# Sigmoid attention inside the ternary feed-forward's steps, VectorE's order in them, and the last stage's weights, first norm and routing beside them

## Chip, cores and metric

The kernel runs on one core of one Trainium2 chip. The metric is the device time of the whole kernel in microseconds (us); lower is better. The core has five engines that each work through their own instructions in order: TensorE (PE: matrix products, with weight loads shown apart as PEld), VectorE (DVE), ScalarE (ACT), GpSimd (POOL) and SyncE (SP), whose queue starts most of the DMAs here. An instruction that needs another engine's result waits for it, and so does everything behind it on its own engine.

## What is computed

A net of four layers, each of a cross attention and a feed-forward, all added to one residual `x` of 2048 tokens by 256 features, with `ctx_2048` as the other input of the attentions. The change touches the last three of these eight parts:

```python
def _rmsnorm(x, g):
    return g * (x * jax.lax.rsqrt(jnp.mean(x * x, axis=-1, keepdims=True) + 1e-8))
def _act_quant(x):
    scale = 127.0 / jnp.clip(jnp.max(jnp.abs(x), axis=-1, keepdims=True), 0.0001, None)
    return jnp.clip(jnp.round(x * scale), -128, 127) / scale
def _ternary_quant(w):
    s = jnp.mean(jnp.abs(w))
    return jnp.round(jnp.tanh(w / (s + 1e-8))) * jnp.arctanh(s)
def _linear_bit(x, w, g):
    return jnp.einsum('bsd,od->bso', _act_quant(_rmsnorm(x, g)), _ternary_quant(w))
def _L2_ffn_ref(x, w1, g1, w2, g2, w3, g3):
    h = jax.nn.silu(_linear_bit(x, w1, g1)) * _linear_bit(x, w2, g2)
    return _linear_bit(h, w3, g3)

def _L3_xattn_ref(Q, K, V):          # per batch of 64 tokens
    score = jax.nn.sigmoid(jnp.einsum('bdn,bdm->bnm', Q, K) / sqrt(dk))
    return jnp.einsum('bvn,bnm->bvm', V, score)

def _L3_ffn_ref(...):                # 8 experts of 176, two per token, and a shared one of 352
    scores = jax.nn.softmax(x @ gate_w.T, axis=-1)
    topk_w, topk_i = jax.lax.top_k(scores, 2)
    h = silu(x @ w_gate[e]) * (x @ w_up[e])
    y = sum over e of combine[:, e] * (h @ w_down[e])
    return y + (silu(x @ sw_gate) * (x @ sw_up)) @ sw_down

x = x + _L2_ffn_ref(_layernorm(x), ...)
x = x + _L3_xattn_ref(_layernorm(x), ctx_2048, ctx_2048)
x = x + _L3_ffn_ref(_layernorm(x), ...)
```

## The kernel before

The residual stays on chip as sixteen tiles `xs[i]` of 128 tokens by 256 features, the context as `cs[i]`. Eight stages, named by letters in `STAGES = "ABCDEFGH"`, run one behind the other; each opens its pools of memory on the left or on the right side of SBUF in turn (`side_of`), so that the weights of the next stage are loaded (`weights`, `load_*`) while one stage runs. Stages A to E are not touched. The planner of the language is free to interleave instructions of neighbouring stages where data and buffers allow it.

**Stage F** (`run_F`, L1238) is the ternary feed-forward. Its section has a schedule by hand (`tc.manual_schedule()`): each engine gets the instructions in the order in which they are written. A tile's work is cut into parts, and in step t the loop at L1384 issues each part for tile t minus its lag, so that several tiles are under way at once. In the order of a tile:

- `deviations` (lag -1): mean and variance on VectorE (`b`, `mv`), a small term, and the power -1/2 on GpSimd (`s`).
- `first_sizes` (lag 0): `xk`, the tile less its mean times each of two gains; its largest magnitudes `am`; then `scales` (L1270): a clamp (L1272), a reciprocal (L1274), the factor `sca` for rounding (L1275) and the factor `dqa` for scaling back (L1277).
- `first_rounding` (0) on ScalarE: `xq`, rounded by adding a large number. `first_transposes` (1) on TensorE, `first_copy` (1) on ScalarE: `xT`.
- `hidden_products` (1) on TensorE: `l`, two products of 1024 columns. `gates` (1) on ScalarE: silu, `sl`. `hidden` (2) on VectorE: `h`.
- `squares` (2) on ScalarE: `junk` and the sum `ss`. `gained` (2) on GpSimd: `xr`, `h` times the gain `g3` (L1344). `second_norm` (3): VectorE and a power on GpSimd (`rr`).
- `second_rounding` (3) on VectorE: the largest magnitude `amb` (L1355), `scales` for 128x1, and `hq` (L1358). `second_transposes` (4), `second_copy` (4): `hqT`, `hT`. `output` (4): `op`. `summed` (5) on VectorE: adds into `xs[i]` (L1380).

The banks of PSUM (`xqT`, `l0`, `l1`, `hqT0`, `hqT1`, `op`) are there once each, so a part waits for the readers of its bank of the step before.

**Stage G** (`run_G`, L1397) is the sigmoid attention, tile by tile: norm into `q` on VectorE, transposed context `cT` (copied by VectorE, L1409), scores of two batches of 64 tokens (L1415), sigmoid on ScalarE (L1419), product `gop` (L1425), and the add into `xs[i]` on VectorE (L1428).

**Stage H** (`run_H`, L1451) is the mixture of experts, in four groups of four tiles. `routed` norms and transposes a group, computes the gate products `hgp`, a softmax and the two largest (`softmax_small`, `top2`), and spreads the weights of the experts over `share` in three bf16 pieces; a product with the constant pattern `owner` brings them to the columns (`cb`). The body computes for 14 chunks `pgate` and `pup`, silu, the product `hm`, and collects `hout`. `routed` of the next group is issued whole behind chunk 5. `owner` (a memset and six selections on GpSimd, L1460 to L1464) is built at the head of the stage; H's weights lie on the side that F used.

Of the kernel before, what the change touches and what calls it, by code (L numbers as in the profile page):

```python
# [31 lines left out]
def tile_net(ctx: ExitStack, tc: tile.TileContext, a: dict, out: bass.AP):  # L32
# [31 lines left out]

    beside = []
    pending = []

    def side_of(stage):
        return ("left", "right")[STAGES.index(stage) % 2]


# [1166 lines left out]
    def run_F(w, side):  # L1238
# [3 lines left out]

        if "ternary" in shared:
            with tc.tile_pool(name="Fp0", bufs=1, space=PSUM) as psum:
                for _ in shared.pop("ternary")(side, psum):
                    pass
        at = shared["atanh"]
        t1, t2, t3 = (t.rearrange("p (c n) -> p c n", c=c) for t, c in zip(shared["tern"], (2, 2, 8)))
        with tc.tile_pool(name="Ft", bufs=1, side=side) as tpool, tc.tile_pool(
# [6 lines left out]
            st = [{} for _ in range(NT)]  # L1256

            def deviations(i):

                b6 = pool.tile([P, 6], F32, name="b6")  # L1260
                V.bn_stats(b6, xs[i])
                mv = st[i]["mv"] = pool.tile([P, 2], F32, name="mv")
                V.bn_aggr(mv, b6)
                ve = pool.tile([P, 1], F32, name="ve")
                V.tensor_scalar(ve, mv[:, 1:2], 1e-5, 1e-8, ALU.add, ALU.mult)
                V.tensor_tensor(ve, ve, mv[:, 1:2], ALU.add)
                s = st[i]["s"] = pool.tile([P, 1], F32, name="s")
                G.tensor_tensor(s, ve, mhalf[:, 0:1], ALU.pow)

            def scales(am, s, at_, n, nm):  # L1270

                V.tensor_scalar(am, am, s, 1e-4, ALU.mult, ALU.max)  # L1272
                sc = pool.tile([P, n], F32, name=f"sc{nm}")
                V.reciprocal(sc, am)  # L1274
                V.tensor_scalar(sc, sc, s, 127.0, ALU.mult, ALU.mult)  # L1275
                dq = pool.tile([P, n], F32, name=f"dq{nm}", bufs=4)
                V.tensor_tensor(dq, am, at_, ALU.mult)  # L1277
                return sc, dq

            def first_sizes(i):  # L1280
# [6 lines left out]
                sc, d["dq"] = scales(am, d["s"], at[:, 0:2], 2, "a")  # L1287
                d["xk"], d["sc"] = xk, sc
# [57 lines left out]
            def second_norm(i):  # L1346
                d = st[i]
                V.tensor_scalar(d["ss"], d["ss"], 1.0 / 1024.0, 1e-8, ALU.mult, ALU.add)
                d["rr"] = pool.tile([P, 1], F32, name="rr")
                G.tensor_tensor(d["rr"], d["ss"], mhalf[:, 0:1], ALU.pow)  # L1350

            def second_rounding(i):
                d = st[i]
                am = pool.tile([P, 1], F32, name="amb")
                V.tensor_reduce(am, d["xr"], AX.X, ALU.max, apply_absolute_value=True)  # L1355
                sc, d["dqb"] = scales(am, d["rr"], at[:, 2:3], 1, "b")
# [25 lines left out]

            deviations(0)
            for t in range(NT + 6):  # L1384
                for part, lag in (
                    (summed, 5), (first_transposes, 1), (first_copy, 1), (second_transposes, 4), (second_copy, 4),
                    (hidden, 2), (hidden_products, 1), (gates, 1), (second_norm, 3), (squares, 2), (gained, 2),
                    (first_sizes, 0), (first_rounding, 0), (second_rounding, 3), (output, 4), (deviations, -1),
                ):
                    if 0 <= t - lag < NT:  # L1390
                        part(t - lag)

# [38 lines left out]
    def load_H(wp):  # L1431
# [16 lines left out]
        w["down"] = t  # L1448
        return w

    def run_H(w, side):  # L1451


        with ExitStack() as es:
            cp = es.enter_context(tc.tile_pool(name="Hc", bufs=1, side=side))
            pool = es.enter_context(tc.tile_pool(name="Hw", bufs=2, side=side))
            psum = es.enter_context(tc.tile_pool(name="Hp", bufs=1, space=PSUM))

            owner = cp.tile([96, 1408], BF, name="owner")
            G.memset(owner, 1.0)  # L1460
            for t in range(3):
                rows = owner[32 * t : 32 * t + 32]
                G.affine_select(rows, rows, [[1, 1408]], ALU.is_ge, 0.0, base=0, channel_multiplier=-176)
                G.affine_select(rows, rows, [[-1, 1408]], ALU.is_ge, 0.0, base=175, channel_multiplier=176)  # L1464
            shares = []
            for b in range(2):
                t = cp.tile([96, 512], BF, name=f"share{b}")
                V.memset(t, 0.0)
                shares.append(t)

            def routed(g):

                ids = range(4 * g, 4 * g + 4)
                xnT = norm_T(pool, psum, ids)
                gp = psum.tile([P, 4, 8], F32, tag="tp", name="hgp")
                for j in range(4):
                    for c in range(2):
                        PE.matmul(
                            gp[:, j, :], xnT[:, c, j * P : (j + 1) * P], w["gate"][:, c, :], start=c == 0, stop=c == 1
                        )  # L1480
                sc = softmax_small(pool, gp, 4, 8)
                (s1, s2), _ = top2(pool, sc, 4, 8)
                V.tensor_tensor(s1, s1, s2, ALU.add)
                comb = pool.tile([P, 4, 8], F32, name="comb")
                V.tensor_tensor(comb, sc, s1, ALU.mult)
                tp = psum.tile([P, 4, P], F32, tag="tp", name="combT")
                for j in range(4):
                    PE.transpose(tp[0:8, j, :], comb[:, j, :], ident)
                src = tp[0:8].rearrange("e j t -> e (j t)")
                sh = shares[g % 2]  # L1490
                r = pool.tile([8, 512], F32, name="shr")
# [154 lines left out]
```

## Time and profile before

| | us |
|---|---|
| median of 3 runs | 2878.74 (2876.58 to 2881.87) |
| the profiled execution | 2879.53, its span 2877.8 |
| TensorE, VectorE, ScalarE, GpSimd busy | 2468.2, 1914.5, 1531.7, 1506.4 |
| stages A to E | up to 2346.9 |
| F, from the first tile's statistics | 2346.9 to 2495.3 |
| G | 2495.3 to 2555.2 |
| H | 2555.2 to 2877.8 |

The page gives for each engine its busy time, the span in 40 slices with tenths of busy time, the clock that TensorE was granted, the chain of work that ended last, and groups of instructions by line with the mean duration of one and the idle time before them. The bounds of the stages in the table were read from the chain: the last row of one stage's lines and the first of the next. A stage's limit is read from its own stretch, since a share of the whole span mixes all eight. In the stretches table a row gives start and end, length, and for each engine busy time and number of instructions, then the granted clock and the DMA share. Busy times of one engine can overlap a little where two instructions overlap; start-to-start times add up.

### The profile page before, as it was taken

To read this page: it belongs to the slowest core of one execution; us is meant where nothing else is said; L and a number is where in the kernel's file an instruction comes from. 1 tells how busy PE (TensorE), PEld (TensorE's weight loads), DVE (VectorE), ACT (ScalarE), POOL (GpSimd) and SP (SyncE) were. 2 spreads that over 40 slices of the span, in tenths; PEclk is the share of its full clock that TensorE was granted. 3 is DMA by queue.
4 is the path that set the end of the run, shared out by engine and by line. 5 is a ranking of instruction groups with operands and counts; after the bars stand their busy time and mean duration, and the time that the engine had idled before them with its cause. 6 is when DMAs were issued, how large, how long until landed. Compare 5 with 4: busy or idle time off the path is not lost.

```text
span 2877.8 us, 44432 instructions
## 1 busy us (share of the span) xinstructions
PE 2468.2 (86%) x16072; PEld 1449.1 (50%) x16072; DVE 1914.5 (67%) x3989; ACT 1531.7 (53%) x2145; POOL 1506.4 (52%) x1681
## 2 busy tenths in 40 slices
PE   4989798777778777689999999789888976789999
PEld 2545344344444444346666666556555533445555
DVE  7877554699999999775455455663577669833332
ACT  1657221599999999655555555353345556521110
POOL 4655433588888888665555555311587754400000
PEclk9999899999999999889999999888999988999999
DMA  6553000499999999910000000001443300200000
GB/s 166 128 116 70 23 1 1 106 202 203 202 207 201 204 201 199 186 59 8 15 15 15 8 1 1 30 30 24 103 93 89 92 1 1 76 1 8 8 8 8
DMA packets 610599, 223.70 MB, mean 78 GB/s; under 512 B 547366, under 2 KB 600524, under 8 KB 605772
## 3 DMA queue, kind: packets, MB, share of 16 engines
q1 hardware_dynamic: 607308, 220.07, 35.0%
q8 instruction: 127, 2.08, 0.3%
q10 hardware_dynamic: 3072, 0.79, 0.2%
q14 instruction: 92, 0.75, 0.1%
HBM read 66.91 MB, written 18.87 MB: 30 GB/s over the span
## 4 chain that ended last, share of the span: by engine, by line
PE 50%; DVE 22%; issue 9%; POOL 5%; ACT 2%; DMA 1%; ACTq 0%; DVEq 0%; POOLq 0%; SPq 0%
DVE e L789 11%; PE yp L985 4%; PE ppq L926 3%; PE ppk L926 3%; PE hout L1502 3%; PE vp L914 3%; PE pgate L1523 3%; PE pup L1523 3%; PE sp L944 2%; PE ep L1072 2%; PE op L970 2%; PE hmp L1065 2%; PE sc L759 1%; PE op L495 1%; POOL e L286 1%
## 5 line engine op out<-in xcount | busy, mean ns | idle before, releaser
L813 ACT ACTIVATE ei<-e,nb,sq 128x2048 int16<-128x2048 f32 x256 | 535.4, 2092 | 43.4 <-DVE nb L810 39.7
L823 POOL CAST eb<-ei 128x2048 bf16<-128x2048 int16 x256 | 482.5, 1895 | 116.1 <-ACT ei L813 102.0
L759 PE MATMUL sc<-kT,qz 128*128 128x512 bf16 x1024 | 298.1, 382 | 142.0 <-DVE e L789 139.9
L246 DVE TENSOR_REDUCE negm<-s 128x2 f32<-128x512 f32 (+1 forms) x512 | 300.9, 611 | 130.6 <-PE s L242 127.4
L789 DVE TENSOR_SCALAR_CACHE_REDUCE e<-sc,mx 128x1024 f32<-128x1024 f32 x256 | 326.1, 1274 | 0.8 <-DVE nb L810 0.7
L789 DVE TENSOR_SCALAR_CACHE_REDUCE e<-sc 128x1024 f32<-128x1024 f32 x256 | 312.4, 1220 | 10.5 <-PE sc L759 10.5
L278 ACT ACTIVATE e<-s 128x1024 f32<-128x1024 f32 (+1 forms) x256 | 233.2, 915 | 152.8 <-PE s L274 117.3
L242 PE MATMUL s<-stk,stq 96*128 96x256 bf16 (+1 forms) x1024 | 192.2, 271 | 41.2 <-DMA d3k<-t3k 24.8
L759 PEld LDWEIGHTS <-qz 128*128 128x128 bf16 x1024 | 94.9, 97 | 261.2 <-issue 202.6
L934 POOL TENSOR_TENSOR rwq<-rwq,sin 128x512 f32<-128x512 f32 x64 | 81.1, 1268 | 240.1 <-ACT rwq L931 203.7
L274 PE MATMUL s<-stq,stk 128*128 128x256 bf16 (+1 forms) x1024 | 180.6, 262 | 10.8 <-DMA stq<-nm 5.4
L772 PEld LDWEIGHTS <-vz 128*64 128x64 bf16 x4096 | 123.2, 110 | 114.0 <-issue 113.9
L946 DVE TENSOR_REDUCE mx<-sp 128x4 f32<-128x512 f32 x64 | 44.3, 692 | 192.7 <-PE sp L944 192.7
L772 PE MATMUL av<-eT,vz 128*64 128x128 bf16 x4096 | 164.0, 223 | 7.3 <-DMA eT<-eb 7.2
L87 POOL TENSOR_TENSOR rstd<-ve,mhalf 128x1 f32<-128x1 f32 (+1 forms) x56 | 42.4, 757 | 240.9 <-DVE ve L85 145.9
L931 ACT ACTIVATE rwq<-ppq,dbq 64x512 f32<-64x512 f32 x128 | 87.4, 683 | 148.9 <-DVE rtq L928 148.0
L1533 DVE TENSOR_TENSOR hm<-pup,sl 128x512 f32<-128x512 f32 (+1 forms) x56 | 38.7, 692 | 191.1 <-PE pup L1523 187.4
L242 PEld LDWEIGHTS <-stq 96*128 96x128 bf16 x1024 | 93.6, 101 | 131.9 <-issue 108.6
L296 PE MATMUL o<-e,vmo 128*32 128x256 f32 (+1 forms) x2048 | 151.1, 367 | 7.4 <-POOL e L286 6.0
L1531 ACT ACTIVATE sl<-pgate 128x512 f32<-128x512 f32 (+1 forms) x56 | 33.4, 597 | 219.2 <-PE pgate L1523 219.1
L286 POOL TENSOR_SCALAR_AFFINE_SELECT e<-e 128x256 f32<-128x256 f32 (+1 forms) x256 | 133.2, 547 | 31.0 <-ACT e L278 30.3
L914 PE MATMUL vp<-Dwv,hnT 128*128 128x512 f32 x256 | 123.8, 605 | 4.0 <-ACT hnT L889 4.0
(349 smaller groups left out, 5518.5 us busy)
## 6 DMA issues: line engine op xcount, KB each, us to landing
stk<-d3k SPq DMA_DIRECT2D x96, 192.0 KB
stq<-d3q SPq DMA_DIRECT2D x96, 192.0 KB
d3k<-t3k SPq DMA_DIRECT2D x160, 64.0 KB
d3q<-t3q SPq DMA_DIRECT2D x96, 64.0 KB
eT<-eb SPq DMA_TRANSPOSE x256
fw<-in_L_ffn_w SPq DMA_DIRECT2D x3, 1024.0 KB
x<-in_x SPq DMA_DIRECT2D x16, 128.0 KB
c<-in_ctx SPq DMA_DIRECT2D x16, 128.0 KB
```

Of the source, the lines that this page charges most:

```text
L242: PE.matmul(sc[:, hh, lo:hi], qs[0:96, 2 * hp + hh, qc * P : (qc + 1) * P], ks[0:96, 2 * hp + hh, lo:hi], start=band is None, stop=True, s ...
L246: V.tensor_reduce(negm[:, qc, 2 * hp : 2 * hp + 2], sc[:, :, lo:hi], AX.X, ALU.max, negate=True)
L274: PE.matmul(sc[:, c, lo:hi], ks[:, h, lc * P : (lc + 1) * P], qs[:, h, lo:hi], start=True, stop=True)
L278: S.activation(e[:, :, lo:hi], sc[:, :, lo:hi], AF.Exp, scale=scale)
L759: PE.matmul(sc[:, k0 : k0 + 512], qz[i % 2][:, h, :], kT[:, h // 2, 1024 * part + k0 : 1024 * part + k0 + 512], start=True, stop=True,)
L772: PE.matmul(av[i][r0 : r0 + 64, h // 4, :], vz[:, kt, h // 4, h % 4, :], eT[:, kt, :], start=h == 0 and kt < 2, stop=h == H - 1 and kt >= ...
L789: V.tensor_scalar(e, scs.pop((n, part)), 1.0, mx[:, 0:1] if part else LOWEST, ALU.mult, ALU.max, accum_out=mx[:, part : part + 1],)
L813: S.activation(ei, es_.pop(n), AF.Exp, bias=nb, scale=sq[i][:, h : h + 1], accum_out=sums[i][:, h : h + 1],)
L823: G.tensor_copy(eb, eis.pop(n - 1))
L914: PE.matmul(vp, hnT[g][:, c, j * P : (j + 1) * P], wv[:, c, :], start=c == 0, stop=c == 1)
L926: PE.matmul(pp, wt[:, c, hh * P : (hh + 1) * P], hnT[g][:, c, :], start=c == 0, stop=c == 1)
L1523: PE.matmul(pp[:m], w[nm + "s"][:, c, cols], xnT[:, c, :], start=c == 0, stop=c == 1)
```

## The change

The sigmoid attention G becomes parts of F's steps (`g_...`), trailing by five to seven tiles; `SEQ` drops the letter G from the order of the stages, so H takes the other side of memory and its weights are loaded from the end of E on. Sigmoid is written by tanh, with half of the context's row sums added (`half`). G's norm and its add go to GpSimd, its copy to ScalarE. In F the factors of the norms are formed before they are needed, so that `scales` has one operation less, and the parts have another order. H's `owner` is built piece by piece in the steps, and `routed` becomes a generator `routed_H`, whose first group is issued in the last steps of F and whose later groups are spread over chunks from the third on.

```diff
+    SEQ = STAGES.replace("FG", "F")
...
+            U = 1e-4 / 127.0
+            base = [[tpool.tile([P, n + 1], F32, name=f"base{nm}{b}") for b in range(2)] for nm, n in (("a", 2), ("b", 1))]
...
+            def first_factors(i):
+                mv, t = st[i]["mv"], base[0][i % 2]
                 ve = pool.tile([P, 1], F32, name="ve")
-                V.tensor_scalar(ve, mv[:, 1:2], 1e-5, 1e-8, ALU.add, ALU.mult)
-                V.tensor_tensor(ve, ve, mv[:, 1:2], ALU.add)
-                s = st[i]["s"] = pool.tile([P, 1], F32, name="s")
-                G.tensor_tensor(s, ve, mhalf[:, 0:1], ALU.pow)
+                V.tensor_scalar(ve, mv[:, 1:2], 1e-5, 1e-8 * U * U, ALU.add, ALU.mult)
+                V.scalar_tensor_tensor(t[:, 2:3], mv[:, 1:2], U * U, ve, ALU.mult, ALU.add)
+                st[i]["fa"] = factors(t, 2, "a")
+
+            def factors(t, n, nm):
+                r = pool.tile([P, 1], F32, name=f"r{nm}")
+                G.tensor_tensor(r, t[:, n : n + 1], mhalf[:, 0:1], ALU.pow)
+                f = pool.tile([P, n + 1], F32, name=f"f{nm}")
+                G.tensor_scalar(f, t, r, 1.0, ALU.mult, ALU.mult)
+                return f
+
+            def scales(am, f, n, nm):
+                V.tensor_scalar(am, am, 1.0 / 127.0, f[:, n : n + 1], ALU.mult, ALU.max)
                 sc = pool.tile([P, n], F32, name=f"sc{nm}")
                 V.reciprocal(sc, am)
-                V.tensor_scalar(sc, sc, s, 127.0, ALU.mult, ALU.mult)
                 dq = pool.tile([P, n], F32, name=f"dq{nm}", bufs=4)
-                V.tensor_tensor(dq, am, at_, ALU.mult)
+                V.tensor_tensor(dq, am, f[:, 0:n], ALU.mult)
...
+            def second_factors(i):
+                d, t = st[i], base[1][i % 2]
+                V.tensor_scalar(t[:, 1:2], d["ss"], U * U / 1024.0, U * U * 1e-8, ALU.mult, ALU.add)
+                d["fb"] = factors(t, 1, "b")
+
+            def second_sizes(i):
...
+                V.tensor_reduce(d["am"], d["xr"], AX.X, ALU.max, apply_absolute_value=True)
...
+            def g_norm(i):
...
+                V.tensor_scalar(ve, mv[:, 1:2], 1e-5, None, ALU.add)
+                rstd = pool.tile([P, 1], F32, name="grstd")
+                G.tensor_tensor(rstd, ve, mhalf[:, 0:1], ALU.pow)
+                V.tensor_scalar(mv[:, 0:1], mv[:, 0:1], -1.0, None, ALU.mult)
+                d["q"] = pool.tile([P, D], F32, name="gq")
+                G.tensor_scalar(d["q"], xs[i], mv[:, 0:1], rstd, ALU.add, ALU.mult)
+
+            def g_context(i):
...
+                d["ctp"] = psum.tile([P, 2, 2, P], F32, tag="xqT", name="gcT")
...
+            def g_context_copy(i):
...
+                S.copy(d["cT"], d["ctp"][:, 0])
...
+                S.activation(junk, cs[i], AF.Identity, scale=0.5, accum_out=d["half"])
+
+            def g_scores(i):
...
+                    sp = psum.tile([P, 4, P], F32, tag=f"hqT{b}", name=f"gsp{b}").rearrange("p (n a) t -> p n (a t)", n=2)
...
+            def g_tanh(i):
...
+                    S.activation(sg, d["sp"][b], AF.Tanh, scale=0.0625)
...
+            def g_product(i):
...
+                d["gop"] = psum.tile([P, D], F32, tag="op", name="gop")
...
+            def g_sum(i):
...
+                S.activation(y, d["gop"], AF.Identity, scale=0.5, bias=d["half"])
+                G.tensor_tensor(xs[i], xs[i], y, ALU.add)
+
+            parts = [
+                (summed, 5), (first_transposes, 1), (first_copy, 1), (second_transposes, 4), (second_copy, 4),
+                (second_factors, 3), (first_sizes, 0), (hidden, 2), (g_product, 7), (g_sum, 7), (hidden_products, 1),
+                (gates, 1), (squares, 2), (gained, 2), (g_context, 6), (g_context_copy, 6), (first_rounding, 0),
+                (second_sizes, 3), (deviations, -1), (g_deviations, 5), (second_rounding, 3), (first_factors, -1),
+                (g_norm, 5), (g_scores, 6), (g_tanh, 6), (output, 4),
+            ]
             deviations(0)
-            for t in range(NT + 6):
-                for part, lag in (
-                    (summed, 5), (first_transposes, 1), (first_copy, 1), (second_transposes, 4), (second_copy, 4),
-                    (hidden, 2), (hidden_products, 1), (gates, 1), (second_norm, 3), (squares, 2), (gained, 2),
-                    (first_sizes, 0), (first_rounding, 0), (second_rounding, 3), (output, 4), (deviations, -1),
-                ):
-                    if 0 <= t - lag < NT:
+            first_factors(0)
+            for t in range(NT + 8):
+                for part, lag in parts:
+                    if 0 <= t - lag < NT and (with_g or not part.__name__.startswith("g_")):
                         part(t - lag)
+                    if with_g and t >= 8 and part.__name__ == "gained":
+                        next(heads.get("owner", head), None)
+
+                    if with_g and t >= NT + 2 and "H" in heads:
+                        head = heads.pop("H")(pool, psum, ("l0", "l1"), "xr")
+                    if t >= NT + 3 and part.__name__ in ("first_copy", "gained"):
+                        next(head, None)
...
+    def owners(owner):
+        G.memset(owner, 1.0)
+        yield
+        for t in range(3):
+            rows = owner[32 * t : 32 * t + 32]
+            G.affine_select(rows, rows, [[1, 1408]], ALU.is_ge, 0.0, base=0, channel_multiplier=-176)
+            yield
+            G.affine_select(rows, rows, [[-1, 1408]], ALU.is_ge, 0.0, base=175, channel_multiplier=176)
+            yield
+
+    def routed_H(w, g, pool, psum, tags, big):
+        xnT, sh = w["xnT"][g % 2], w["share"][g % 2]
+        if g < 2:
+            G.memset(sh, 0.0)
...
-                    if ch == 5 and g + 1 < NG:
-                        nxt = routed(g + 1)
+                    if ch == 3 and g + 1 < NG:
+                        nxt = routed_H(w, g + 1, pool, psum, ("tp", "tp"), "xn4")
+                    next(nxt, None)
```

In `routed_H` the code of `routed` is cut by nine `yield`s: behind the statistics, behind half of the norm, behind its end, behind each of two groups of transposes (`hnT0`, `hnT1`), behind the gate products, behind the softmax, behind the combination, and behind the last pieces of `share`. The four `base` tiles hold the factors `watanh` times a constant and, in their last column, the mean square; they are filled during E.

## The prediction

> **What bounds the kernel now.** I read the stretches table first, cut where the chain of waits changes its character: F's first five steps, its eleven full steps, its last five, stage G, H's head, H's body.
>
> ```profile
> core 0: us, PE busy (x) PEld busy (x) DVE busy (x) ACT busy (x) POOL busy (x), PEclk, DMA share, GB/s
> 2346.90:2380.00 33.10, 19.62 (x64) 8.67 (x64) 28.74 (x80) 18.09 (x31) 12.10 (x13) 0.61 0.00 0
> 2380.00:2478.40 98.40, 60.86 (x320) 36.66 (x321) 92.38 (x253) 59.77 (x102) 42.40 (x46) 0.90 0.00 1
> 2478.40:2495.30 16.90, 12.48 (x67) 7.43 (x64) 13.62 (x29) 8.36 (x14) 6.56 (x7) 0.80 0.00 0
> 2495.30:2555.20 59.90, 48.98 (x288) 27.68 (x288) 28.62 (x85) 18.67 (x33) 13.56 (x11) 1.00 0.31 91
> 2555.20:2562.30 7.10, 4.55 (x25) 3.63 (x26) 3.42 (x12) 2.77 (x5) 0.00 (x0) 0.86 0.00 0
> 2562.30:2877.80 315.50, 311.16 (x1029) 182.47 (x1028) 95.57 (x211) 49.76 (x83) 11.46 (x14) 0.99 0.02 7
> ```
>
> In F VectorE is busy 92.4 of 98.4 us and sets the pace, 98.4/11 = 8.95 us a step. In G and H TensorE does. The chain of waits says how G spends its 59.9 us:
>
> ```profile
> 2540.58 1.13 PE sp L1415 x8
> 2541.73 0.61 ACT sg L1419
> 2542.38 1.57 PE gop L1425 x8
> ...
> 2544.32 1.13 PE sp L1415 x8
> ```
>
> One tile every 3.74 us: scores, sigmoid, product in a row, nothing else to do meanwhile. H's body is TensorE at 311 of 315.5 us, so only its 7.1 us head can shrink. Then the timeline of one F step, VectorE with GpSimd's long operation, and one early pair:
>
> ```profile
> 2445.93 2.49 POOL L1344 TENSOR_TENSOR xr<-h,fg 128x512 f32<-128x512 f32 x2
> ...
> 2446.97 0.25 DVE L1272 TENSOR_SCALAR am<-am,s 128x2 f32<-128x2 f32 x1
> ...
> 2447.45 0.99 DVE L1275 TENSOR_SCALAR sca<-sca,s 128x2 f32<-128x2 f32 x1
> ...
> 2357.99 2.46 DVE L1284 SCALAR_TENSOR_TENSOR xk<-x,mv,fg 128x256 f32<-128x256 f32 x2
> ```
>
> `sca` needs 0.23 us when GpSimd is idle and 0.99 here: it ends as `xr` ends at 2448.42. The pair `xk` takes 0.87 alone and 2.46 under an `xr`. So some VectorE operations stand still under GpSimd, 0.76 us of each full step. Reductions, statistics and operations with a PSUM input run on beside it, and so do 128x1 operations (L1272 took 0.21 us under an `xr` at 2486.05).
>
> **The change, part by part.** Stages A to E keep their instruction order on every engine; only F, G and H's head count.
>
> *VectorE's step.* By start-to-start times of the full step 2443.69 to 2452.44: `x` 0.40, `base` of the second norm 0.07, `xk` pair 0.79, reduction 0.78, scale, reciprocal and `dqa` 0.56, `h` pair 1.32, reduction `amb` 1.14, two pairs of statistics 1.12 (one is G's), scale, reciprocal and `dqb` 0.57, `hq` 0.66, four small ones 0.41. Sum **7.8 us**, against 8.95. Gone are both L1275 (0.91 with its stall, and 0.13); `h` now stands behind `first_sizes`, so `xr` runs under reductions and statistics. What is late next is `hq`: it comes 2.8 us behind `h`, while `xr` needs 2.5 us from its own start and now stands behind `g_sum`'s add, which waits for ScalarE's `gy`. I add 0.6 to 1.0 us for it and 0.3 for `xk` and the 128x2 scale meeting GpSimd's small operations: about 9.1.
>
> *GpSimd's step.* Three powers at 0.55, two small factor multiplies, the q norm at 0.57 (L679, same form), the add at 0.75 (L500), `xr` 2.54: 6.1 us. The factor multiply has no row; L698 on 128x16 gives 0.27, L679 0.57, I take 0.27 by size; not below zero, since it is an extra instruction. Seven steps add an `owner` piece at 1.35 (L1463; the memset 1.27), hidden in G before: 7.4 us. It stands ahead of the first factors and the q norm and in front of `xk`'s port: between 0 and 1.35, I take 0.4 a step, as GpSimd has 1.7 us to spare but VectorE none.
>
> A rule of the Trainium skill speaks against this part: GPSIMD Engine Reference, section Engine selection, puts elementwise work on VectorE and calls GpSimd about two times slower for two inputs. The rows agree for the add (0.75 against 0.42 at L1428), hardly for the norm (0.57 against 0.41). By the rule both stay on VectorE: 7.8 + 0.8 = 8.6 us before any wait, 9.9 with them. By the rows the loss lies on an engine with spare time.
>
> SBUF — State Buffer, section SBUF: two separate sides, says a GpSimd operation holds the shared port for its whole length and the VectorE one fully blocks. The 0.99 and 2.46 above are that; but the 128x1 rows pass under `xr`. If everything blocked, a step were 7.8 + 6.4 = 14.2 us; by the rows only `hq`, `xk` and the 128x2 ones count, hence 9.1.
>
> *TensorE and ScalarE make a loop.* Time 0 is the end of `h`, when TensorE may write `l`. As in the step before, the gates start at 1.12, `junk` at 2.27, `xq` at 3.39; now `cT` (0.37, L518) and the half sum (about 0.55 + 0.20, between L518 and L1294, plus L1337's accumulator read) go ahead of it, 0.9 net: `xq` 4.3 to 5.4, the two tanh (1.09, the sigmoid's pair) to 6.4. The second bank of `hqT` waits for tanh; `hqT` (1.06) ends at 7.3, `gop` (1.57) at 8.9, the first two `l` at 9.3, and then the next `h` must be done. So this loop closes at **9.3 us**, VectorE's at 9.1. TensorE's own work is 4.7 + 3.1 = 7.8 us of it, so its clock (0.90 in F, 1.00 in G) should stay near full. Tanh has no row beside silu: as sigmoid's 595 ns. A switch of tables is excluded by the changed kernel's order: no table load stands between silu and tanh inside the steps.
>
> I take 9.3 in four full steps and 9.5 in the seven with `owner`: 103.4 us for eleven, **5.0 more** than before.
>
> *The first five steps.* Three of them lose the stall and the small L1275 (0.9 each), the first pays one factor multiply: 33.1 - 2.6 = 30.5.
>
> *The last steps and G.* G no longer follows; it trails F by two tiles. From the loop, with what is gone taken out: step 16 without `xq` and its transposes 8.2, step 17 without `l` and gates 6.4, steps 18 and 19 without `junk` 5.3 each, step 20 without `hT` 4.7 (`gop`, `gy`, `xnT`'s copy, `cT`, half, tanh). Step 21: one transpose group 0.45, `gop` 1.57, `hgp` 2.82: 4.85. Sum 34.75 to the end of `hgp`, for 16.9 + 59.9 before.
>
> *H's head.* From `hgp`'s end: last `gcT` and scores 1.6, tanh to 2.75, table load 1.28 and exp to 4.3, sixteen small VectorE operations at 0.22 to 7.8 (between 2561 and 2570 they are spaced so), `combT` 0.45: 8.3 us, of which TensorE idles 3.9 behind a `combT` that formerly stood behind two rounds of products (2571.75). Before, `hgp`'s end was the start of the body, and 7.1 lay ahead. So most of this gain is given back.
>
> *H's weights.* Twelve loads move on SP's queue from F's end to E's end; behind them stand only the output stores. They landed at 2515 for a use at 2562, hidden before and after; F has DMA share 0.00. Cost none; up to +3 if they meet E's last stacks. The `share` memset leaves VectorE for GpSimd: under 0.3.
>
> Sum: 30.5 + 103.4 + 34.8 + 8.3 = 177.0, against 33.1 + 98.4 + 16.9 + 59.9 + 7.1 = 215.4. **38.4 us less**. From the profiled execution's 2879.5 that gives 2841.1; the median of the runs, 2878.74, lies 0.8 lower: **2840.5**.
>
> **The rivals.** Outside the full steps 43.4 us are saved, so each case is a length of the full step.
> - *The loops overlap better.* The half sum and `cT` fit into ScalarE's waits, `hq` escapes `xr`: 8.3 us, 11 x (8.3 - 8.95) = -7, total 2828. For it: every engine's own work is below 8. Against: four in-order engines, each waiting for two others.
> - *The loops lengthen each other.* `xr` starts late because `gy` is late, `hq` and so `hqT` follow: 11 us, +22.6, total 2858. For it: both loops are within 0.3 us. Against: VectorE may lead by a step's buffers.
> - *Slower: the port.* If GpSimd's operations shut out nearly all of VectorE, the step is 14.2 and the time 2879.5 - 43.4 + 57.8 = 2894 (2893 against the median). It decides from 12.9 us a step, that is if VectorE stands still for 5.1 of GpSimd's 6 to 7 us. The pair at 2357.99 speaks for it, the 128x1 rows and the reductions against it.
> - *It doesn't do what it says*: G stays serial because `gop` waits for each tanh. That is in the loop already; alone it would give a step of 8.95 + 3.74 = 12.7, no change.
>
> **How the numbers follow.** Forecast 55%, better overlap 22%, lengthened 17%, slower 4%, no change 2%. Factor multiply and tanh move the step by at most 0.5 us (6 in all), the tail by 6; with the two neighbours this gives 2822 to 2862. Repeats of this kernel lie 0.2% apart, so that is what can be told from no change. Faster 94%, same 2%, slower 4%.
>
> **What would show it.** F's full steps (between two `summed`) at 9.2 to 9.6; no long 128x2 row; `hq` at 1.3 to 1.7 instead of 0.75; no tanh stretch after F; `hgp` about 35 us after step 16 starts; an idle TensorE of 4 us ahead of `combT`; H's body at 315. Wrong it is if full steps are above 11, if a table load appears among them, or if `xk` again shows 1 us or more.

## The result and the profile after

The changed kernel takes **2838.38 us** (median of 4 runs, 2835.05 to 2846.52), beside 2879.16 (2876.58 to 2881.87) for the kernel before: ratio 0.9862, interval 0.984 to 0.9885. The forecast was 2840.5. The profiled execution is the slowest of the four, 2846.52 with a span of 2844.8, so the comparison of the traces has to leave out what the change doesn't touch. Stages A to E have the same work in the kernels before and after but for the four small fills of `base`, yet their end differs by up to 10 us between profiled executions: F's first statistics of the second tile start at 2350.25 in the trace of before, 2352.90 in that of after, and from 2344.90 to 2354.79 in the others. So I measure from that row to the end: 527.6 us before, 491.9 after, **35.7 us less**.

The stretches table of the changed kernel is cut as before: F's first five steps, its eleven full steps, from step 16 to the end of the last `hgp` of the first group, H's head, H's body. Columns are start and end, length, then busy time with number of instructions of each engine.

```profile
core 0: us, PE busy (x) PEld busy (x) DVE busy (x) ACT busy (x) POOL busy (x), PEclk, DMA share, GB/s
2352.90:2382.63 29.73, 21.35 (x64) 9.00 (x64) 21.50 (x64) 16.73 (x28) 13.75 (x20) 0.52 0.59 176
2382.63:2480.91 98.28, 76.15 (x480) 43.62 (x480) 91.62 (x264) 75.79 (x157) 76.35 (x104) 1.00 0.00 1
2480.91:2519.94 39.03, 30.50 (x200) 19.52 (x200) 24.68 (x75) 23.68 (x54) 20.61 (x30) 0.91 0.00 1
2519.94:2530.64 10.70, 3.92 (x22) 1.89 (x22) 4.99 (x24) 4.32 (x9) 1.76 (x2) 0.88 0.00 1
2530.64:2844.80 314.16, 310.31 (x1024) 182.75 (x1024) 87.58 (x177) 48.34 (x75) 9.43 (x12) 0.99 0.02 7
```

With the same cuts the trace of before has 29.8, 97.3, 77.9, 7.1 and 315.5. The full steps do a tile of attention more and last 1.0 us longer in all; GpSimd is busy 76.4 us in them instead of 42.4, TensorE 76.2 instead of 60.0, and TensorE's clock rises from 0.89 to 1.00. VectorE is busy for as long as before (91.6 for 91.3): the stall on L1275 went, G's statistics and other stalls came. The gain is the third row, 38.9 us: G has no stretch of its own any more. The head gives 3.6 back. H's weights cost nothing to see: the load runs at DMA share 0.59 beside the first five steps, which last as long as before.

A step without an `owner` piece (step 7), then a full step with one, then the last one with one (step 14), then a place in the last steps, in the timeline of VectorE and GpSimd (start, duration, engine, line, operation, in brackets the idle time before it and what ended it):

```profile
2403.98 2.50 POOL L1368 TENSOR_TENSOR xr<-h,fg 128x512 f32<-128x512 f32 x2
...
2405.21 1.82 DVE L1384 TENSOR_SCALAR hq<-xr,scb 128x1024 f32<-128x1024 f32 x1
...
2441.38 1.35 POOL L1571 TENSOR_SCALAR_AFFINE_SELECT owner<-owner 32x1408 bf16<-32x1408 bf16 x1
2441.47 1.81 DVE L1384 TENSOR_SCALAR hq<-xr,scb 128x1024 f32<-128x1024 f32 x1
...
2443.69 0.55 POOL L1290 TENSOR_TENSOR ra<-basea,mhalf 128x1 f32<-128x1 f32 x1 [0.95 <-DVE gmv L1424]
...
2445.73 0.43 DVE L1297 TENSOR_SCALAR am<-am,fa 128x2 f32<-128x2 f32 x1
...
2447.89 2.50 POOL L1368 TENSOR_TENSOR xr<-h,fg 128x512 f32<-128x512 f32 x2
...
2469.99 1.02 POOL L91 TENSOR_TENSOR rstdh<-ve,mhalf 128x4 f32<-128x4 f32 x1
2471.05 0.41 DVE L95 TENSOR_SCALAR xn<-x,mvh,rstdh 128x256 f32<-128x256 f32 x1 [2.42 <-POOL rstdh L91]
2471.38 0.75 DVE L1384 TENSOR_SCALAR hq<-xr,scb 128x1024 f32<-128x1024 f32 x1
...
2503.74 1.06 DVE L95 TENSOR_SCALAR xn<-x,mvh,rstdh 128x256 f32<-128x256 f32 x3 [1.76 <-POOL rstdh L91]
2504.71 0.48 DVE L1406 SCALAR_TENSOR_TENSOR x<-op,dqb,x 128x256 f32<-128x256 f32 x1
```

Three things are to be seen. `hq` is long: in step 7 it takes 1.82 us for 0.75 under `xr`. From step 8 on `xr` is about over when `hq` comes, but the `owner` piece starts 0.09 us ahead of it, directly behind `xr` in GpSimd's queue, and `hq` takes 1.81. In both cases it ends 0.55 us after the GpSimd operation. While `hq` stands under `owner`, GpSimd itself waits 0.95 us for the small operations behind it. And at the last full step but one VectorE idles for 2.42 us: the norm of one of H's later groups (`xn`, L95; the first group's writes `xr`) stands in VectorE's queue ahead of `hq`, moved there by the planner (H by hand, below, has none there), and it waits for `rstdh`, which stands behind `xr` and `owner`. That step took 11.27 us; the other six with a piece 8.87 to 9.30, those without one 7.97 to 8.66. In the last two lines the norm of a later group again holds up the add `x` of F in the tail. The kernel before has such a step too: in its step 8, 10.40 us long where most take 8.74, G's norm waits in the same way, so the 97.3 us hold about 1.7 of it.

```profile
2412.39 0.41 DVE L91 TENSOR_SCALAR q<-x,mv,rstd 128x256 f32<-128x256 f32 x1 [2.01 <-POOL rstd L87]
```

TensorE in the last steps and the head:

```profile
2505.24 1.09 PE L1467 MATMUL gop<-gsg,cT 128*64 128x256 f32 x8 [1.79 <-DVE x L1406]
...
2511.49 1.98 PE L1467 MATMUL gop<-gsg,cT 128*64 128x256 f32 x8 [2.74 <-DVE x L1406]
...
2528.25 1.01 PE L1609 MATMUL combT<-ident,comb 128*8 128x128 f32 x4 [4.73 <-DVE comb L1605]
2530.64 3.78 PE L1655 MATMUL pgate<-xnT,hwgate 128*128 128x512 f32 x4 [1.38 <-DVE shr L1614]
```

`gop` waits twice for an add of F that frees its bank `op`; the first of these adds is the one at 2504.71 above, behind H's norm. Then TensorE idles 4.73 us for the routing and another 1.38 for `shr`, since `combT` uses a bank of F's pool and `pgate` gets its banks when that pool closes.

### The profile page after: what moved, and what is told of

Its sections match the earlier page's. It is cut to its first block, busy times and chain, and to the rows that moved or that the text cites. A ratio compares the mean times of both kernels' runs of the same rounds, so it can differ in the third digit from the quotient of the medians.

```text
span 2844.8 us, 44419 instructions
## 1 busy us (share of the span) xinstructions
PE 2456.3 (86%) x16072; PEld 1442.3 (51%) x16072; DVE 1885.7 (66%) x3939; ACT 1543.1 (54%) x2200; POOL 1543.2 (54%) x1759
## 4 chain that ended last, share of the span: by engine, by line
PE 48%; DVE 21%; issue 9%; POOL 7%; ACT 3%; DMA 1%; ACTq 0%; SPq 0%; POOLq 0%; DVEq 0%
DVE e L793 11%; PE yp L989 4%; PE vp L918 4%; PE ppq L930 4%; PE pgate L1655 3%; PE ppk L930 3%; PE hout L1631 3%; PE pup L1655 3%; POOL e L290 2%; PE sp L948 2%; PE ep L1076 2%; PE op L974 2%; PE hmp L1069 2%; PE sc L763 1%; PE op L499 1%
## 5 line engine op out<-in xcount | busy, mean ns | idle before, releaser
L938 POOL TENSOR_TENSOR rwq<-rwq,sin 128x512 f32<-128x512 f32 x64 | 81.1, 1268 | 241.3 <-ACT rwq L935 216.3
L278 PE MATMUL s<-stq,stk 128*128 128x256 bf16 (+1 forms) x1024 | 179.6, 261 | 11.4 <-DMA stq<-nm 5.0
```

Source lines behind the costliest of these rows:

```text
L278: PE.matmul(sc[:, c, lo:hi], ks[:, h, lc * P : (lc + 1) * P], qs[:, h, lo:hi], start=True, stop=True)
```

## The experiments

The theory at the start: F's new order and factors shorten the step, G fills waits of engines that had time, `owner` costs VectorE `hq`'s stall, and the tail is longer than it must be because of where H's first group stands. The rivals: that the order of parts doesn't matter, that GpSimd is the wrong engine for G's norm and add (only the add was moved), that the tanh form is only decoration. All kernels, in us; the stretches are first five steps, eleven full steps, step 16 to the first `pgate`, and the body:

| kernel | median | ratio to before (interval) | stretches | sum |
|---|---|---|---|---|
| before | 2879.16 | | 29.8, 97.3, 85.0, 315.5 | 527.6 |
| after | 2838.38 | 0.9862 (0.984 to 0.9885) | 29.7, 98.3, 49.7, 314.2 | 491.9 |
| G apart | 2858.66 | 0.993 (0.9911 to 0.9948) | 28.6, 80.0, 81.1, 315.0 | 504.7 |
| former order | 2858.37 | 0.9935 (0.9916 to 0.9955) | 29.8, 114.4, 51.1, 314.0 | 509.4 |
| owner late | 2839.11 | 0.9869 (0.9846 to 0.9891) | 29.7, 94.8, 50.6, 313.8 | 488.9 |
| add on VectorE | 2842.85 | 0.9873 (0.9855 to 0.9891) | 29.8, 96.4, 50.4, 314.8 | 491.3 |
| shares late | 2836.68 | 0.9854 (0.9838 to 0.9871) | 28.5, 98.3, 42.2, 315.0 | 484.0 |
| sigmoid | 2855.34 | 0.9919 (0.9902 to 0.9935) | 28.5, 112.0, 48.7, 314.2 | 503.3 |
| H by hand | 2833.74 | 0.9843 (0.9828 to 0.9858) | 28.6, 95.6, 42.6, 315.0 | 481.8 |
| combined | 2829.42 | 0.9827 (0.9813 to 0.9842) | 28.7, 94.3, 43.4, 314.6 | 480.9 |
| combined, by hand | 2828.85 | 0.9827 (0.9813 to 0.984) | 28.9, 92.4, 36.1, 320.4 | 477.8 |

Each ratio is to executions of before that were timed beside the kernel; stretches and sum are those of one execution each. The first stretch differs by 1.2 us between kernels that do the same work in it; I read nothing below that from a sum. The full steps of shares late, the same code as after, took 98.3 us again. By their intervals G apart, former order and sigmoid are slower than after; owner late, add on VectorE, shares late and H by hand can't be told from it, so what is said of these four rests on the stretches.

**G apart.** F keeps its new factors and order, G is a stage of its own again:

```diff
-    with_g = "FG" in STAGES
-    SEQ = STAGES.replace("FG", "F")
+    with_g = False
+    SEQ = STAGES
```

> F with its new factors and order, but the sigmoid attention as a stage of its own behind it, owner built at H's head and H's first group issued there. My theory: the new order alone takes the stall and the two small operations out of VectorE's step, 8.95 to about 7.3 us (7.8 less G's 0.7, and xr no longer behind gy), 11 steps give -18, so about 2859; the sigmoid stretch of 60 us stands behind F again. Rival: the reorder brings nothing by itself since TensorE and ScalarE close a loop as long as VectorE's: 2877 to 2880.

504.7 us: 22.9 of the 35.7 come from F's new factors and order (with H's later groups spread over chunks), 12.8 from G inside the steps with what goes with it, `owner` and H's first group there and H's weights earlier. The full steps last 6.6 to 8.1, most of them 7.23. The timeline of one step:

```profile
2434.26 1.40 DVE L1353 SCALAR_TENSOR_TENSOR h<-l,dqa,sl 128x512 f32<-128x512 f32 x2
...
2435.24 2.50 POOL L1368 TENSOR_TENSOR xr<-h,fg 128x512 f32<-128x512 f32 x2
...
2437.68 0.75 DVE L1384 TENSOR_SCALAR hq<-xr,scb 128x1024 f32<-128x1024 f32 x1
```

`hq` starts 0.06 us before `xr` ends and is not lengthened; between `h` and `hq` stand only reductions and statistics. That is the order at its best, 1.5 us a step below the 8.74 of most steps before. Putting G in takes the full steps from 80.0 to 98.3 and the rest from 81.1 to 49.7.

**Former order.** The changed kernel with its parts in the order of before, G's parts put in at their lags: `hidden` ahead of `first_sizes`, `second_factors` and `first_factors` late.

```diff
-                (second_factors, 3), (first_sizes, 0), (hidden, 2), (g_product, 7), (g_sum, 7), (hidden_products, 1),
-                (gates, 1), (squares, 2), (gained, 2), (g_context, 6), (g_context_copy, 6), (first_rounding, 0),
+                (hidden, 2), (g_product, 7), (g_sum, 7), (hidden_products, 1), (gates, 1), (second_factors, 3),
+                (squares, 2), (gained, 2), (g_context, 6), (g_context_copy, 6), (first_sizes, 0), (first_rounding, 0),
...
```

> The changed kernel with the parts in the former order: hidden ahead of first_sizes, gained ahead of first_sizes, statistics at the end of the step, G's parts beside. My theory: xr then runs under the xk pair, the 128x2 scale and dqa, which stand still for it, 0.4 to 0.8 us a full step, and hq still meets owner; 2842 to 2848. Rival: the order is worth nothing, as VectorE meets GpSimd somewhere in any case: 2836 to 2840.

It lost more than I expected: 16.1 us in the full steps, 17.5 in all. One step in the timeline:

```profile
2435.57 0.72 POOL L1475 TENSOR_TENSOR x<-x,gy 128x256 f32<-128x256 f32 x1 [1.75 <-ACT gy L1474]
...
2436.33 0.43 DVE L86 BATCH_NORM_STATS2 bnst<-x 128x6 f32<-128x256 f32 x1 [1.33 <-POOL x L1475]
...
2437.13 2.50 POOL L1368 TENSOR_TENSOR xr<-h,fg 128x512 f32<-128x512 f32 x2
2437.37 1.05 DVE L1297 TENSOR_SCALAR am<-am,fa 128x2 f32<-128x2 f32 x1
...
2438.54 1.10 DVE L1301 TENSOR_TENSOR dqa<-am,fa 128x2 f32<-128x2 f32 x1
```

Two 128x2 operations stand under the two halves of `xr`, 1.05 us for 0.23 and 1.10 for 0.14. In most full steps of the kernel before only the second of two stood, 0.25 and 0.99 (0.64 and 0.99 in one). New is the add ahead of `xr` on GpSimd: ScalarE's `gy` is late, `xr` with it, and H's hoisted statistics wait 1.33 us for the add. So part of the loss is H's hoisting, and it wasn't separated. In the middle four of the eleven full steps (8.91 to 10.07 us) the two operations aren't lengthened; `hq` is, in three of them (1.78 to 1.92). By median this kernel and G apart are equal (2858.37 and 2858.66), by sum it is 4.7 us behind. The fourth case, the former order with G apart and the new factors, wasn't run, so what G in the steps brings under the former order stays open.

**Owner late.** The pieces of `owner` come only from step 16 on:

```diff
-                    if with_g and t >= 8 and part.__name__ == "gained":
+                    if with_g and t >= 16 and part.__name__ == "gained":
```

> The changed kernel with the seven pieces of owner in the steps from 16 on instead of 8 on. My theory: in steps 8 to 14 hq stands still for the piece, 1.8 us instead of 0.75, and the step is 9.05 instead of 8.0; without it -7 us, 2830 to 2833, full steps of 8.0 to 8.3. Rival (the forecast's term): GpSimd's spare time hides most of a piece, 0.2 to 0.4 a step: 2835 to 2838.

Six steps that had a piece (8 to 13) fall from a mean of 9.06 to 8.39, so a piece costs 0.67 us, half of its 1.35. I expected twice the gain in the sum. The timeline of VectorE and GpSimd shows why no more is to be had, and below it TensorE's `l` in this step and the one before:

```profile
2437.57 0.72 POOL L1475 TENSOR_TENSOR x<-x,gy 128x256 f32<-128x256 f32 x1 [0.64 <-ACT gy L1474]
2438.26 2.50 POOL L1368 TENSOR_TENSOR xr<-h,fg 128x512 f32<-128x512 f32 x2
...
2440.27 0.51 DVE L1301 TENSOR_TENSOR dqb<-amb,fb 128x1 f32<-128x1 f32 x1
2440.70 0.74 DVE L1384 TENSOR_SCALAR hq<-xr,scb 128x1024 f32<-128x1024 f32 x1
...
2428.58 2.05 PE L1338 MATMUL l<-tern,xT 128*128 128x512 bf16 x8
...
2437.71 1.45 PE L1338 MATMUL l<-tern,xT 128*128 128x512 bf16 x6 [0.29 <-DVE h L1353]
```

`hq` is short again, but VectorE now meets the end of `xr` one operation earlier, in `dqb` (0.51 to 1.01 for 0.14), and `xr` in turn is held by the add, which waits for `gy`, ScalarE's copy of TensorE's `gop`. The steps alternate between 8.23 and 8.55; in those of 8.23 TensorE's `l` waits 0.29 us for `h`, in those of 8.55 not at all: the loop of TensorE and ScalarE is as long as VectorE's step now. Steps 8 to 14 gain 5.0 us in all (60.6 for 65.6), step 15 gives 1.6 of it back (9.55 for 7.98) and the tail 0.9.

**Add on VectorE.** The add of `g_sum` on the engine that the rule in the prediction names:

```diff
-                G.tensor_tensor(xs[i], xs[i], y, ALU.add)
+                V.tensor_tensor(xs[i], xs[i], y, ALU.add)
```

> The changed kernel with g_sum's add on VectorE instead of GpSimd, behind h. By the skill's rule for elementwise work: 0.42 on VectorE instead of 0.75 on GpSimd, xr starts earlier, time same or down to 2832. My theory by the rows: VectorE is the bound, so the add's 0.4 us a step is paid in full, and it has two inputs in SBUF and stands just where xr starts, so it waits for the first half of xr: +0.4 to +1.6 us in each of 16 steps, 2845 to 2863.

491.3 against 491.9: neither the rule nor my rows decide, and the 0.4 to 1.6 us a step that I expected to lose were not lost. The timeline:

```profile
2433.33 2.67 POOL L1368 TENSOR_TENSOR xr<-h,fg 128x512 f32<-128x512 f32 x2
2433.82 1.05 DVE L1475 TENSOR_TENSOR x<-x,gy 128x256 f32<-128x256 f32 x1
...
2437.61 0.75 DVE L1384 TENSOR_SCALAR hq<-xr,scb 128x1024 f32<-128x1024 f32 x1
```

VectorE pays 1.05 us for the add, because it stands under `xr` (0.42 alone), but GpSimd starts `xr` right behind `h`, so `owner` is over when `hq` comes, which gets its 1.05 back. Moving an operation moved the collision.

**Sigmoid.** The same kernel with the sigmoid function itself, and so without the half sum on ScalarE:

```diff
-                    S.activation(sg, d["sp"][b], AF.Tanh, scale=0.0625)
+                    S.activation(sg, d["sp"][b], AF.Sigmoid, scale=0.125)
```

> The changed kernel with sigmoid itself in the steps, product without the half sum. Each step then switches ScalarE's table twice. By the trace a load takes 1.28 us: ScalarE's loop of 8.2 becomes 8.2 - 0.6 + 2.6 = 10.2 us, so about +1.2 in seven full steps, +2.2 in four, +2 in seven last ones: 517 to 525 from F's first statistics to the end instead of 491.9. By the price that ScalarE: Activation LUTs states, 2.66 us a switch: 13 us a step, 550 to 560, which is slower than before the change (527.6). Rival: one set holds sigmoid and silu, no loads, and the missing half sum saves: 488 to 492.

ScalarE's timeline of one step:

```profile
2433.07 0.38 ACT L1471 ACTIVATE gy<-gop 128x256 f32<-128x256 f32 x1 [1.14 <-PE gop L1464]
2433.48 1.28 ACT L1347 ACT_TABLE_LOAD   x1
2434.77 1.27 ACT L1347 ACTIVATE sl<-l,dqa 128x512 f32<-128x512 f32 x2
...
2438.34 1.28 ACT L1455 ACT_TABLE_LOAD   x1
2439.63 1.09 ACT L1455 ACTIVATE gsg<-gsp 128x512 f32<-128x512 f32 x2
```

Silu and sigmoid load a table in turn, 1.28 us each, and the next ACTIVATE starts 1.29 after the load. The load starts 0.03 us after `gy` ends, so a switch costs ScalarE 1.3 us here. The 2.66 us that the expectation took from the Trainium skill (ScalarE: Activation LUTs, section What ACT_TABLE_LOAD costs) were not seen. The first two full steps have no load yet, the other nine hold 19, or 24.3 us. The full steps grow by 13.7 only, since ScalarE waited 1.6 to 2.0 us in most of them (for `l`), where part of the loads now lies, and the half sum is gone (0.41 a step); the whole grows by 11.4, less than I expected. TensorE's granted clock was 0.91 in these nine steps, where after had 1.00; what that adds wasn't separated. So the tanh form carries nearly all of what G in the steps brings over G apart (12.8).

**Shares late.** `combT` and the share pieces of the first group are issued at the head of H instead of in F:

```diff
+            if g == 0:
+                return
+            shared_out(w, g, pool, psum, tags, comb)
...
+            shared_out(w, 0, pool, psum, ("tp", "tp"), w["comb"])
             nxt = iter(())
```

> The changed kernel with the last piece of H's first routing (combT and share) issued at the head of H's own section instead of inside F's. From the first F statistics to the end the changed kernel took 491.9 us. My theory: there TensorE stands 4.7 us ahead of combT and 1.4 behind it, since the products stand behind combT in its queue; with one round of products ahead of combT the first product starts right behind the last gop, about 7 us earlier, and 1 us comes back at cb: 485 to 487. Rival: the share is late in any case and the products wait for it at cb: 490 to 492.

TensorE in the head:

```profile
2514.47 3.78 PE L1663 MATMUL pgate<-xnT,hwgate 128*128 128x512 f32 x4 [0.65 <-ACT gy L1474]
...
2519.93 0.60 PE L1617 MATMUL combT<-ident,comb 128*8 128x128 f32 x4
...
2524.45 0.38 PE L1667 MATMUL cb<-share,owner 96*128 96x512 bf16 x1 [0.49 <-POOL share L1625]
```

`pgate` starts right behind the last `gop`, `combT` one round later, and the shares are 0.49 us late instead of 4.73 + 1.38: 7.5 us less from step 16 to `pgate`, and 7.9 in the sum, a little more than expected.

**H by hand.** The section of H in its written order, nothing else:

```diff
             psum = es.enter_context(tc.tile_pool(name="Hp", bufs=1, space=PSUM))
+            es.enter_context(tc.manual_schedule())
             owner = w["owner"]
```

> The changed kernel with H's section in the written order too, so that the planner no longer puts norms of H's later groups into VectorE's queue among F's steps. My theory: step 14 loses its 2.3 us wait for rstd, the last steps two waits of 1.8 and 2.7, so 485 to 487 from F's first statistics to the end, with H's body as before at 314. Rival: these norms only fill time, and in the written order H's body waits for each later group's routing, 1 to 3 us a group: 490 to 500.

The stretches table from the full steps on:

```profile
2377.46:2473.05 95.59, 76.15 (x480) 43.61 (x480) 90.74 (x251) 75.69 (x157) 77.91 (x103) 1.00 0.00 1
2473.05:2515.70 42.65, 31.66 (x220) 20.01 (x220) 25.08 (x79) 27.89 (x63) 20.43 (x31) 0.95 0.00 1
2515.70:2830.70 315.00, 311.17 (x1024) 183.05 (x1024) 96.87 (x212) 48.34 (x75) 12.46 (x15) 0.99 0.02 7
```

The 11.27 step is 9.04, the last steps 6.2, 4.6 and 5.8 instead of 7.5, 8.3 and 6.2, and the body needs what it needed (315.0). `hgp` ends 32.5 us after step 16, for 39.0. In VectorE's full steps there are 251 instructions instead of 264: the hoisted norm is gone from them. That was the planner's part: 2.7 us in the full steps and 7.1 behind them. The medians differ by 4.6.

**Combined.** Shares late, `owner` in thirteen pieces, the selections of half the width, behind `second_factors` in steps 2 to 14 (VectorE then runs `h`, which has a PSUM input), and the half sum moved ahead of `gates` on ScalarE:

```diff
-                    if with_g and t >= 8 and part.__name__ == "gained":
+                    if with_g and t >= 2 and part.__name__ == "second_factors":
...
+            for h in range(2):
+                cols = rows[:, 704 * h : 704 * h + 704]
+                G.affine_select(cols, cols, [[1, 704]], ALU.is_ge, 0.0, base=704 * h, channel_multiplier=-176)
...
-                (gates, 1), (squares, 2), (gained, 2), ...
+                (g_half, 6), (gates, 1), (squares, 2), (gained, 2), ...
```

> Three edits on the changed kernel: owner in thirteen half pieces, each between the second factors and g_sum's add where GpSimd waits for gy, in steps 2 to 14; the half sum ahead of the gates, where ScalarE waits for TensorE; combT as in comb_late. My theory: the loop over TensorE and ScalarE falls from 8.2 to 7.7, VectorE's step to 7.9 to 8.2, 11 full steps about 90 instead of 98.3, and 5 to 6 at H's head: 477 to 480 from F's first statistics to the end, ratio to before 0.980 to 0.984. Rival (owner in GpSimd's gap delays xr and so hq by as much as it saves): 484 to 488.

Steps 7 to 13 take 8.47 to 8.55, but the hoisted norm still makes one of 10.61. The sum is 0.9 above what I expected.

**Combined, by hand.** On top of it, H in written order, with two rounds of its products ahead of `combT`:

```diff
+            es.enter_context(tc.manual_schedule())
...
-            shared_out(w, 0, pool, psum, ("tp", "tp"), w["comb"])
+            ahead = [products(w["xnT"][0], 0), products(w["xnT"][0], 1)]
...
+                    if g == 0 and ch == 0:
...
+                        shared_out(w, 0, pool, psum, ("tp", "tp"), w["comb"])
```

> The version with small owner pieces, the half sum ahead of the gates and the routing shares late, and on top of it the last section in its written order, with its first two rounds of gate and up products ahead of the share transposes. From the start of F's first statistics to the end the version without the last two took 480.9 us, and one of its steps still took 10.6 us for 8.53 because a group norm of the last section stood ahead of the scale in VectorE's queue; the same tail in written order brought the changed kernel from 491.9 to 481.8, of which some 2 us is the long step and the rest the last five steps and the head. If the two gains add in part, that is 471 to 477 us here, a ratio near 0.980 to the kernel before, no step of 10.6, and pgate within 10 us of the last hgp. The rival says that the planner's order is needed in the last section once the shares come late: then 478 to 485 us, with VectorE or GpSimd late in the section's body, which was 314 us.

I expected 471 to 477 and got 477.8. All full steps are 8.54 or less and the tail is 36.1, but the body grew by 5.8. TensorE in the head of this kernel, and then the same place in the one above:

```profile
2512.20 1.98 PE L1662 MATMUL pgate<-xnT,hwgate 128*128 128x512 f32 x4 [0.83 <-ACT gy L1476]
...
2519.18 0.60 PE L1621 MATMUL combT<-ident,comb 128*8 128x128 f32 x4
2523.70 0.45 PE L1683 MATMUL cb<-share,owner 96*128 96x512 bf16 x1 [3.92 <-POOL share L1629]
```

```profile
2522.24 0.38 PE L1671 MATMUL cb<-share,owner 96*128 96x512 bf16 x1 [0.48 <-POOL share L1629]
```

In written order TensorE has nothing behind `combT` and waits 3.92 us for the shares; the planner had put a round of products there. `combT` a round earlier might recover that; it wasn't tried. Both combined kernels are faster than before by 1.7% (the intervals are in the table); against the changed kernel they were not timed side by side, and the three intervals meet at 0.984.

## Why the prediction was right, and where its terms were off

The mechanism held: G as a stage vanishes, the full steps stay about as long, most of H's head remains. The sum of the traces is 35.7 us less, the forecast 38.4. That the median came within 2.1 us of the forecast is partly luck. The errors of the terms have both signs: 2.5 us too much gain in the first steps, 4.0 too little in the full steps, 3.1 and 2.4 too much in the tail and the head, 1.3 not foreseen in H's body. And the medians differ by 40.8 where the traces differ by 35.7; stages A to E, whose end varies by 10 us, can make that difference.

- **First five steps**, forecast 2.6 less: 0.1 less (in other executions up to 1.3). I had priced removed stalls as time without asking what is late next; TensorE's granted clock was 0.52 there (0.62 before), but what sets these steps was not tried.
- **Steps without `owner`**, forecast 9.3, by TensorE and ScalarE's loop: 8.4 with all of G and no piece (owner late). Terms of that loop were too long: `xq` starts 4.0 after `h` instead of 4.3, as the half sum costs 0.41 start to start; `hqT` ends at 6.7 instead of 7.3; `gop` takes 1.09 in the steps, not the 1.57 of the trace of G, with which I priced it. The first two `l` end at 8.3. And the first two of the four steps at 9.3 hold only part of G: they took 8.07 and 7.97.
- **`owner`**, forecast +0.4 on VectorE's step and so 9.5 in seven: a piece costs 0.67, and 9.06 is the mean of six. Where it would hurt was wrong: I put it ahead of the factors, it hurts `hq` directly behind `xr` (in one step `dqb` ahead of it).
- **`hq`**, forecast 1.3 to 1.7 under `xr`: in step 7 that came, with 1.82, from step 8 on it is 1.81 to 1.91 under `owner`, or `dqb` takes the stall. With no piece in the steps `hq` stays at 0.74 from step 8 on (owner late), but only because `dqb` meets the end of `xr` first; with G apart both are short. VectorE's own sum, 7.8 + 0.6 to 1.0 + 0.3, gives 8.7 to 9.1, of which I took the upper end.
- **All eleven full steps**, forecast 5.0 more: 1.0 more. The forecast doesn't have the 11.27 step, made 2.2 us longer by H's norm in VectorE's queue; nor did it see that its base, 8.95 a step, held G's norm in the same place (1.7 us), and that its cut at 2478.40 lies 1.1 us behind the end of the last full step. Without these norms the full steps would take 96.1 us for 95.6, about as long as before.
- **Step 16 to `hgp`**, forecast 34.75: 39.0. The planner's hoisting again; with H by hand it is 32.5, so the step by step sum itself was 2 us too long.
- **The head**, forecast 8.3 with TensorE idle for 3.9: 10.7 with 4.73 and 1.38. The idle time was seen; not seen was that `pgate`'s banks hang on a reader of F's pool (`shr`).
- **H's body and weights**, forecast no change: 314.2 for 315.5.
- **Small terms.** The factor multiply took 0.27 (`fb`) as estimated from L698, and 0.62 where `xk` runs beside it (`fa`). "128x1 operations pass" is right for operations with one tensor input (`amb`, 0.18 under `xr`), wrong for those with two from SBUF (`dqb`, up to 1.33 in the changed kernel, under the end of `xr` and `owner`).
- **The rules.** That elementwise work belongs on VectorE cost nothing and brought nothing here (491.3 against 491.9). The lock between GpSimd and VectorE was read too widely: in the Trainium skill, SBUF — State Buffer, section SBUF: two separate sides, which the prediction cites, it concerns VectorE operations in a two-port mode or with two inputs in SBUF only. The rows fit: `dqb` and `dqa`, with two, stand, and reductions and the 128x1 `amb` don't. `hq` and `am` have one tensor input and stand; that they run in a two-port mode is shown by no row here. So the rival of 14.2 us a step asked for more than the page says.

So better overlap was the right rival for what the loops allow (8.3 a step, 8.39 with `owner` late); `owner` and the hoisted norm made 8.93 of it, and the tail and the head gave less than forecast. Its total of 2828 is what the combined kernels reach.

## What to carry to other kernels

Merging a serial stage into the steps of another paid here by the stage's own waits, and the order within the step decided how much: it has to keep the long GpSimd operation beside work that doesn't stand under it. By medians, the kernel with the former order and the one with G apart each reach half of the gain. When the next stage's first work is issued early and its section is left to the planner, look at each in-order queue for an operation of that stage that waits ahead of the current one's: here that cost about 10 us, which a schedule by hand gave back, and the kernel before had such a step as well. An order by hand can also take away fillers: with H by hand alone the body stayed at 315.0, with the shares late on top it grew by 5.8, so waits that the planner had covered have to be covered by hand.

## What the runs showed of the hardware

- A VectorE operation that starts while GpSimd is at work can stand until the end of GpSimd's operation: `hq` starts 0.09 us after `owner` or 1.23 after `xr`, and ends 0.55 after its end in both cases, 1.81 and 1.82 us for 0.75.
- The waiting one can come ahead of GpSimd's next: in add on VectorE the add starts under the first half of `xr` (1.26 us) and ends 0.28 after it, and the second half takes 1.45.
- Which small operations stand under GpSimd's long ones goes by inputs as well as by size: 128x1 with one tensor input 0.18 (`amb`), 128x2 with one 1.05 for 0.23 (`am`), 128x2 with two 1.10 for 0.14 (`dqa`), 128x1 with two 0.51 to 1.33 for 0.14 (`dqb`).
- A switch of ScalarE's tables took 1.28 us (sigmoid), and no load stands between silu and tanh in the steps (after).
- The eight products of `gop` take 1.09 us inside the steps and 1.57 in G and at the end of the tail; no run separates why. TensorE's granted clock was 1.00 in the full steps and 0.89 before, when it was busy for less.
